# Two graph layers on one core: conv taps scaled one part ahead, a re-ordered beginning, and an own row for one channel of the early gates

## The chip, the cores and the metric

The kernel runs on one core of one Trainium2 chip. Its engines are TensorE (PE, with weight loads shown as PEld), VectorE (DVE), ScalarE (ACT), GpSimd (POOL) and SyncE (SP, which only issues transfers here). Each engine works through its own queue of instructions in order; semaphores tie the queues together. The time is device microseconds (us) of one execution; a kernel's time is the median of several.

## The reference

All arithmetic is float32. There are 64 graphs of 256 nodes with 256 features.

```python
# layer 0, then layer norm of x + result
deg = adj.sum(-1); deg = where(deg != 0, deg, 1)
a_plus = deg^-0.5[:, :, None] * adj * deg^-0.5[:, None, :] + alpha * eye
x = layernorm(x + (a_plus @ x) @ W.T + b)

# layer 1, then layer norm of x + result
h = relu(bn1(conv1x1(x)))                 # over channels
h = bn2(conv17(h))                        # 17 taps along the 256 nodes
x_conv = relu(h + x)
s = x @ w_se.T + b_se                     # 3 numbers per node
A = exp(-|s_n - s_m|^2) * adj             # the mask is adj
x_nmp = A @ relu(x @ w_msg.T + b_msg)
gi = concat(x_conv, x_nmp) @ w_ih.T + b_ih;  gh = x @ w_hh.T + b_hh
r, z = sigmoid(gi_r + gh_r), sigmoid(gi_z + gh_z)
n = tanh(gi_n + r * gh_n)
x = layernorm(x + (1 - z) * n + z * x)
```

## The kernel before

**Quarters.** The 64 graphs are worked off in four quarters of Q = 16. The 17-tap convolution is done in the frequency domain: each graph's h is cut into eight overlapping blocks of 48 nodes and transformed by a matmul (`p_dft`) into the tile `VM`, which holds 48 frequencies of 128 blocks, that is of 16 graphs. Then follow the products with the transformed taps (`products`, L559, one step for each of 12 pairs of frequencies, the `u` tiles loaded from memory), the inverse transforms on DVE (`real_transform`, `complex_begin`, `complex_end`), and stores to `xc_d`. After that the quarter's gates run: `gru` forms the gate products `p_g` (L893) from seven sums, and mixes and normalizes the result.

**One graph.** `layer0(g)` is a generator in pieces: degrees on ACT (L363), their power on POOL (L373, `dis`), adjacency transposed (`p_adjT`), the diagonal added on DVE (L387), x scaled (L402), `p_hT`, `p_out`, x<-p_out (L425), and `layernorm`: statistics and variance on DVE, a power on POOL (L329), `ln_mr` on DVE (L332), the normalization on ACT (L334). `layer1(g)` does the transposition of x (`p_x1T`), the 1x1 convolution (`p_conv`), `sq` and its sums on DVE (L467 to L470), `p_msg` and its ReLU, `p_dft`, `p_rows`, `p_dist`, exp on ACT (L521), the weighting `aT` on DVE (L524), and `p_nmp`. `graphs` interleaves: while graph i is in layer 1, graph i+2 is in layer 0 and i+3 begins it, and a third generator ("other") gets a turn at the places that `PLACES` names.

**What the third generator is.** In the first quarter it is `weights(n)`: thirteen parts of the conv taps, one for each of the first graphs. A part is loaded by seven transfers, multiplied by a scale on DVE (L300), transformed by eight matmuls (`p_u`, L308), evicted into `u_set`, subtracted on DVE (L313), added on POOL (L314), and stored to `ud` by three POOL transfers. In later quarters it is the gates of the quarter before: the first four graphs of a quarter ("early", `in_blocks`) run beside the last graphs of the next quarter, the others beside its first graphs and the transforms.

**Early gates.** `transposed(g)` brings the convolution's output into channel order: for early gates and the last quarter DVE transposes it in blocks (L838), POOL adds x (L839), POOL sets the row of x's first channel back to 1 (L840), and ACT applies the ReLU with bn2's bias (L842). That row (channel 0 of `xn`) holds 1 so that biases can ride in the matmuls; before L839 the true channel 0 is loaded over it by SP (L813).

**What sets the order.** A scheduler lays out each engine's queue from the order in which the program is written and from data dependencies. `with tc.issue_after(i):` keeps what is built inside behind instruction i where both are on the same engine. `paced` hands out pieces of one generator behind marked instructions of another. Each tile comes from a pool of a few buffers, so an allocation waits for the release of an older one. In the built program the transfers of SP and ACT share eight completion semaphores: the ninth transfer waits for the first, which holds the issuing queue.

**The beginning.** Loads of graph 0, the batch-norm vectors and graph 1 are issued; `layer0(0)` and `layer0(1)` are merged; `tables` fills the transform's tables by many small DVE copies and 12 transfers; then `batch_norms` makes bn1's and bn2's scales, spreads them by six matmuls with diagonals (`p_norm`, L187) and scales `wc1`.

Of the kernel before, what the change touches and what calls it, by code (L numbers as in the profile page):

```python
# [26 lines left out]
def kernel(  # L27
# [76 lines left out]
    def load(g):  # L104
        if g >= B:
            return
        ain[g] = loads.tile([P, NCH, N], F32, name="adj_t")
        nc.sync.dma_start(ain[g], adj[g].rearrange("(c p) m -> p c m", p=P))
        xin[g] = loads.tile([P, NCH, D], F32, name="x_t")
        nc.sync.dma_start(xin[g], x[g].rearrange("(c p) f -> p c f", p=P))  # L110

# [15 lines left out]
    nc.scalar.copy(warm, neg_half)  # L127
    for i, a in enumerate((bn1_g, bn2_g, bn1_b, bn2_b, bn1_m, bn2_m, bn1_v, bn2_v)):
        (nc.sync if i % 2 else nc.scalar).dma_start(vectors[2 * i : 2 * i + 2], a.rearrange("(c p) -> c p", p=P))
    nc.scalar.dma_start(w0, w0T.rearrange("(k p) o -> p k o", p=P))  # L130
    load(1)
# [31 lines left out]
    bn2_bias = const.tile([P, DCH], F32)  # L163

    def batch_norms(pool):
# [10 lines left out]
        nc.vector.tensor_mul(g, g, v)  # L176
        nc.vector.tensor_mul(m, m, g)
        nc.vector.tensor_sub(b, b, m)
        nc.vector.tensor_copy(bn2_bias, b[:, 2:4])

        ones = pool.tile([P, P], F32, name="ones")
        nc.vector.memset(ones, 1.0)
        rows = [bank("p_norm") for _ in range(2)]
        for i, col in enumerate((g[:, 0:1], g[:, 1:2], b[:, 0:1], b[:, 1:2], g[:, 2:3], g[:, 3:4])):
            diagonal = pool.tile([P, P], F32, name="diagonal", bufs=2)
            nc.vector.tensor_scalar(diagonal, ident, col, None, op0=ALU.mult)
            nc.tensor.matmul(rows[i // 4][:, i % 4 * P : (i % 4 + 1) * P], ones, diagonal, start=True, stop=True)  # L187
# [4 lines left out]
        nc.vector.tensor_copy(wc1[0:1, 0, :D], rows[0][0:1, D:])  # L192
# [22 lines left out]
    def tables(pool):  # L215
# [12 lines left out]
        nc.gpsimd.memset(fwd, 0.0)  # L228
        for r in range(2):
            nc.vector.memset(fwd_row[:, :, 2 * r], 1.0)  # L230
# [9 lines left out]
        with tc.issue_after(DIAGONAL[0]):  # L240

            for r in range(2):
                nc.vector.memset(w_row[:, :, r, NF], (0.5, 1.0)[r])
# [7 lines left out]
        for j in range(GT // 2 + 2):  # L251

            first = NT * (j - 1) - PAD
            lo, hi = max(first, 0), min(first + FL, P)
            nc.sync.dma_start(fwd[lo:hi, j, :], fwd_row[:, lo - first : hi - first])

# [16 lines left out]
    TAPS_OF = {}  # L273

    def load_taps(pool, n):
# [17 lines left out]
        nc.sync.dma_start(tp[KT - 1 :], taps(GC - 1, TR, 1, 1))  # L293

    def weights(pool, n, scale):
# [4 lines left out]
        nc.vector.tensor_mul(tp, tp, scale[:KT].unsqueeze(1).to_broadcast([KT, ng, D]))  # L300
# [3 lines left out]
        for i in range(2):  # L304
# [7 lines left out]
            if i == 1:  # L312
                nc.vector.tensor_sub(us[3], us[1], us[0])  # L313
                nc.gpsimd.tensor_tensor(us[2], us[0], us[1], op=ALU.add)  # L314
                for d, u in zip(ud, (us[0], us[3], us[2])):
                    nc.gpsimd.dma_start(d[:, n * ng : (n + 1) * ng], u)
            yield

    def layernorm(y, eps=LN_EPS, normed=None):

        chunks = range(y.shape[1])
        st = small.tile([P, NCH, nc.vector.BN_STATS_DIM], F32, name="ln_st")
        mv = small.tile([P, NCH, nc.vector.BN_AGGR_DIM], F32, name="ln_mv")
        rs = small.tile([P, NCH], F32, name="ln_rs")
        for c in chunks:
            nc.vector.bn_stats(st[:, c, :], y[:, c, :])
            nc.vector.bn_aggr(mv[:, c, :], st[:, c, :])
        nc.vector.tensor_scalar(rs[:, : len(chunks)], mv[:, : len(chunks), 1], eps, None, op0=ALU.add)  # L328
# [3 lines left out]
        nc.vector.scalar_tensor_tensor(mr[:, : len(chunks)], mv[:, : len(chunks), 0], -1.0, rs[:, : len(chunks)], op0=ALU.mult, op1=ALU.mult)  # L332
# [16 lines left out]
    EVICTED, RELU, SQUARED, AGGREGATED, LAYER0 = {}, {}, {}, {}, {}  # L349
    ADJT, X1, X_SCALED, DIAGONAL = {}, {}, {}, {}  # L350


    def layer0(g):
# [19 lines left out]
        nc.gpsimd.tensor_tensor(dis, deg, neg_half[:, :NCH], op=ALU.pow)  # L373
        adeg = small.tile([P, NCH], F32, name="adeg")
        nc.vector.tensor_scalar(adeg, deg, alpha_t, None, op0=ALU.mult)
# [27 lines left out]
        nc.gpsimd.tensor_tensor(x_t, x_t, b0_t.unsqueeze(1).to_broadcast([P, NCH, D]), op=ALU.add)  # L403

        yield
        hT = work.tile([P, DCH, N], F32, name="hT", bufs=1)
# [23 lines left out]
        yield from layernorm(x1, normed=NORMED)  # L430
# [354 lines left out]
    GATE, CONV, SUMS, OWN = {}, {}, {}, {}  # L785
# [22 lines left out]
    def load_gate(g):  # L808
        inputs = GATE[g] = gate.tile([P, 3 * DCH, N], F32, name="inputs")
        nc.sync.dma_start(inputs[:, : 2 * DCH], xn_d[g])  # L810
        if in_blocks(g):
            with nc.allow_non_contiguous_dma("one channel"):
                nc.sync.dma_start(inputs[0:1, 0], x1_d[g // Q][g % Q][:, 0:1].rearrange("n d -> d n"))  # L813
# [19 lines left out]
    def transposed(g):  # L833
# [3 lines left out]
        if in_blocks(g):  # L837
            behind(nc.vector.transpose(xcT.rearrange("p k (s r) -> p k s r", r=RB), CONV.pop(g)))  # L838
            nc.gpsimd.tensor_tensor(xcT, xcT, inputs[:, 0 : 2 * DCH : 2 * DCH - 1], op=ALU.add)  # L839
            JOINED.append(nc.gpsimd.memset(inputs[0:1, 0], 1.0).ins)  # L840
            for k in range(DCH):
                nc.scalar.activation(xcT[:, k], xcT[:, k], AF.Relu, bias=bn2_bias[:, k : k + 1])  # L842
# [25 lines left out]
    def normed(g, part, y):  # L868
# [8 lines left out]
    def gru(g):  # L877
# [37 lines left out]
        if following:  # L915
            transposed(g + 1)
# [343 lines left out]
```

## Time and profile before

| what | us |
|---|---|
| median of three runs (2070.37 to 2078.38) | 2074.39 |
| the profiled execution | 2077.37 |
| its span | 2075.6 |
| PE busy in the span | 1993.8 |
| DVE, ACT, POOL busy | 1360.7, 972.6, 663.4 |
| first `p_conv` starts at | 34.10 |
| last matmul group starts at | 2062.01 |

A profile line of a time line gives start, duration, engine, source line, operation, output <- inputs, sizes and count; the bracket is the engine's idle time before it and what ended it. A line of the list of waits gives who waited for whom, total us, times and the longest. In both, a name stands for all buffers of that name.

### The profile page before, as it was taken

The page shows a single profiled execution, that of the slowest core. Times are in us where ns is not written, and L with a number is a line of the kernel's source. Part 1 is how long each engine was busy: PE and PEld are TensorE (multiplying, and loading weights), DVE is VectorE, ACT ScalarE, POOL GpSimd, SP SyncE. Part 2 cuts the span into 40 slices and gives each one's busy share as a digit, 9 for nine tenths or more (in the row PEclk, how much of TensorE's full clock was granted, in tenths as well). Part 3 has the DMA queues.
Part 4 walks back from the last instruction along what each step waited for, and adds up shares of the span by engine and source line. Part 5 has one row for each costly group of instructions (what it writes and reads, how often), then busy time and mean ns, then how long its engine had stood idle before and what let it go on. Part 6 is the DMA issues. An engine that isn't in the chain of part 4 may idle for free.

```text
span 2075.6 us, 26338 instructions
## 1 busy us (share of the span) xinstructions
PE 1993.8 (96%) x8157; PEld 1445.7 (70%) x8157; DVE 1360.7 (66%) x3192; ACT 972.6 (47%) x2283; POOL 663.4 (32%) x672
## 2 busy tenths in 40 slices
PE   6989999999999999999999999999999999999997
PEld 5877788888667766777777766677767865555554
DVE  5434457587456788764455778775444899977776
ACT  3656664477442234556654223456655223333333
POOL 3433421022432234223332224323232034434442
PEclk9999999999999999999999999999999999999999
DMA  3765656544437655343334664434333944543431
GB/s 103 235 187 173 182 189 221 178 148 159 111 111 220 188 145 148 112 127 105 120 97 154 214 191 128 116 126 138 97 87 92 298 128 124 146 104 99 97 89 58
DMA packets 268936, 298.04 MB, mean 144 GB/s; under 512 B 84192, under 2 KB 211252, under 8 KB 268798
## 3 DMA queue, kind: packets, MB, share of 16 engines
q1 hardware_dynamic: 208846, 200.37, 33.2%
q10 hardware_dynamic: 44480, 67.39, 9.1%
q0 software_dynamic: 15472, 28.61, 6.4%
q8 instruction: 66, 1.08, 0.2%
q14 instruction: 72, 0.59, 0.1%
HBM read 193.19 MB, written 103.06 MB: 143 GB/s over the span
## 4 chain that ended last, share of the span: by engine, by line
PE 75%; DVE 12%; DMA 5%; ACT 3%; issue 2%; SPq 1%; POOL 1%; ACTq 0%; POOLq 0%; DVEq 0%
PE p_g L893 34%; PE p_k L559 10%; PE p_nmp L533 5%; PE p_hT L410 5%; PE p_out L420 4%; PE p_conv L457 4%; PE p_msg L478 3%; PE p_dft L496 3%; PE p_u L308 2%; PE p_dist L520 2%; PE p_x1T L440 1%; DMA u<-ud 1%; DMA taps<-in_conv2T_dram 1%; DMA inputs<-x_d 1%; PE p_adjT L384 1%
## 5 line engine op out<-in xcount | busy, mean ns | idle before, releaser
L893 PE MATMUL p_g<-wall,sums 128*128 128x384 f32 x1536 | 533.8, 488 | 2.8 <-DVE G L918 1.7
L893 PEld LDWEIGHTS p_g<-wall,sums 128*128 128x128 f32 x1536 | 284.9, 190 | 187.9 <-issue 9.5
L893 PE MATMUL p_g<-wall,inputs 128*128 128x384 f32 x1152 | 405.4, 487 | 6.9 <-DVE G L911 6.9
L893 PEld LDWEIGHTS p_g<-wall,inputs 128*128 128x128 f32 x1152 | 216.7, 190 | 157.4 <-DVE G L911 12.8
L864 POOL TENSOR_TENSOR sums<-inputs 128x384 f32<-128x384 f32 x128 | 141.8, 1108 | 332.3 <-PE p_g L893 309.5
L329 POOL TENSOR_TENSOR ln_rs<-ln_rs,neg_half 128x2 f32<-128x2 f32 x129 | 96.5, 748 | 458.7 <-DVE ln_rs L328 331.0
L524 DVE TENSOR_TENSOR aT<-aT,adjT 128x512 f32<-128x512 f32 x64 | 46.1, 720 | 253.5 <-ACT aT L521 253.5
L559 PE MATMUL p_k<-u,VM 128*128 128x256 f32 x736 | 171.3, 383 | 3.7 <-DMA u<-ud 2.4
L403 POOL TENSOR_TENSOR x_t<-x_t,b_t 128x512 f32<-128x512 f32 x64 | 89.1, 1392 | 249.4 <-ACT x L402 178.5
L559 PEld LDWEIGHTS p_k<-u,VM 128*128 128x128 f32 x736 | 139.6, 192 | 26.8 <-ACT ab L605 3.1
L410 PE MATMUL p_hT<-adjT,x 128*128 128x256 f32 x512 | 128.5, 396 | 13.3 <-ACT x L402 11.8
L533 PE MATMUL p_nmp<-aT,msg 128*128 128x256 f32 x512 | 125.3, 389 | 13.8 <-DVE aT L524 13.8
L937 ACT ACTIVATE G<-G 128x512 f32<-128x512 f32 x128 | 80.5, 631 | 123.7 <-DVE G L962 86.4
L334 ACT ACTIVATE x_g<-x_g,ln_mr,ln_rs 128x256 f32<-128x256 f32 x128 | 70.0, 593 | 137.8 <-DVE ln_mr L332 133.5
L420 PE MATMUL p_out<-w,hT 128*128 128x256 f32 x512 | 123.7, 385 | 7.8 <-ACT hT L415 7.6
L457 PE MATMUL p_conv<-wc,xn 128*128 128x259 f32 x512 | 124.6, 385 | 1.1 <-issue 1.1
L478 PE MATMUL p_msg<-wmsg,xn 128*128 128x256 f32 x512 | 121.3, 379 | 0.0
L533 PEld LDWEIGHTS p_nmp<-aT,msg 128*128 128x128 f32 x512 | 98.9, 194 | 30.7 <-DVE aT L524 16.9
L420 PEld LDWEIGHTS p_out<-w,hT 128*128 128x128 f32 x512 | 96.2, 192 | 30.8 <-ACT hT L415 13.8
L410 PEld LDWEIGHTS p_hT<-adjT,x 128*128 128x128 f32 x512 | 93.3, 195 | 34.5 <-ACT x L402 17.9
L864 POOL TENSOR_TENSOR sums<-inputs,sums 128x384 f32<-128x384 f32 x64 | 79.0, 1234 | 116.2 <-PE p_g L893 115.7
L496 PE MATMUL p_dft<-fwd,h 128*128 128x240 f32 x512 | 114.3, 366 | 0.0
(163 smaller groups left out, 3496.3 us busy)
## 6 DMA issues: line engine op xcount, KB each, us to landing
u<-ud SPq DMA_DIRECT2D x284, 256.0 KB
xn_d<-xn ACTq DMA_DIRECT2D x64, 512.0 KB
inputs<-xn_d SPq DMA_DIRECT2D x64, 512.0 KB
ud<-u_set POOLq DMA_DIRECT2D x39, 480.0 KB, 5.4
adj_t<-in_adj_dram SPq DMA_DIRECT2D x64, 256.0 KB
x_t<-in_x_dram SPq DMA_DIRECT2D x64, 256.0 KB
x_d<-x ACTq DMA_DIRECT2D x64, 256.0 KB
xc_d<-VM SPq DMA_DIRECT2D x64, 256.0 KB
```

What stands on the lines that cost most here:

```text
L329: nc.gpsimd.tensor_tensor(rs[:, : len(chunks)], rs[:, : len(chunks)], neg_half[:, : len(chunks)], op=ALU.pow)
L403: nc.gpsimd.tensor_tensor(x_t, x_t, b0_t.unsqueeze(1).to_broadcast([P, NCH, D]), op=ALU.add)
L410: nc.tensor.matmul(p[:, k, :], x1[:, mc, k * P : (k + 1) * P], adjT[:, mc, 1 - mc : 3 - mc, :].rearrange("p n q -> p (n q)"), start=mc == ...
L420: nc.tensor.matmul(p[:, c, :], hT[:, k, c * P : (c + 1) * P], w0[:, k, :], start=k == 0, stop=k == DCH - 1)
L457: nc.tensor.matmul(p, x1T[:, k, c * P : (c + 1) * P], wc1[:, k, :], start=k == 0, stop=k == DCH - 1)
L478: nc.tensor.matmul(p[:, c, :], x1T[:, k, c * P : (c + 1) * P], wmsg[:, k, :], start=k == 0, stop=k == DCH - 1)
L496: nc.tensor.matmul(p[:, t0 * FL : t1 * FL], h[:, c, k * P : (k + 1) * P], fwd[:, first : first + t1 - t0, :].rearrange("p t f -> p (t f)") ...
L533: nc.tensor.matmul(p[:, k, :], msg[:, mc, k * P : (k + 1) * P], aT[:, mc].rearrange("p n q -> p (n q)"), start=mc == 0, stop=mc == NCH - 1,)
L559: nc.tensor.matmul(p[:, j * D : (j + 1) * D], v[:, k, :], u[:, k, :], start=k == 0 and j == 0 and not onto, stop=k == DCH - 1, skip_group_ ...
L864: nc.gpsimd.tensor_tensor(S[i], x, y, op=op)
L893: nc.tensor.matmul(p[:, : 3 * HD] if k == 0 else p[:, HD:], a[:, k], wall[:, b, k].rearrange("p t d -> p (t d)"), start=first and k == 0, ...
L937: nc.scalar.activation(rz, rz, AF.Tanh, scale=0.5)
```

## The change

- **Taps.** `weights(n)` scales part n+1 behind `aT` of graph n instead of part n at its own start; only part 0 is scaled by itself. The set's subtraction, addition and stores become a third piece, behind degrees and `dis` of graph n+3. The first part starts one place later. x of graph i+3 is loaded behind the last transfer of the taps; adjacency is loaded on its own.
- **Beginning.** Graph 1's adjacency is loaded before the batch-norm vectors, which go over ACT, POOL and SP; the batch norms' first half comes right after both graphs' degrees, with the diagonals in `VM`; the table fill stands behind the second graph's diagonal, its last part behind the scaling of `wc1`; graph 1's normalization moves into the first graph. Two biases go through a small tile and a POOL copy.
- **Layer norm.** `ln_mr` stands behind the next graph's `adeg`, one piece sooner than the normalization, which no longer waits for `sq`.
- **Early gates.** x's first channel is loaded into a row of its own and added on POOL (1 x 256); the row of ones stays; the bias of channel 0 is one less (`less_one`). The DVE transposition stands behind the latest `aT`, one piece of `gru` sooner, and the ReLU behind the latest exp.
- **First quarter.** The real transform and the beginnings of the complex one stand behind the graphs' `sq`, diagonal and `aT`.
- **Last graph.** Half of its first row of results is mixed before the last product, so that half is left behind it.

```diff
+    load_adj(1)
     for i, a in enumerate((bn1_g, bn2_g, bn1_b, bn2_b, bn1_m, bn2_m, bn1_v, bn2_v)):
-        (nc.sync if i % 2 else nc.scalar).dma_start(...)
+        (nc.scalar if i < 2 else nc.gpsimd if i < 5 else nc.sync).dma_start(...)
+    load_x(1)
...
+        with tc.issue_after(DIAGONAL[1]):
+            nc.vector.tensor_mul(g, g, v)
...
+            for i, col in enumerate((g[:, 0:1], g[:, 1:2], b[:, 0:1], b[:, 1:2], g[:, 2:3], g[:, 3:4])):
+                nc.vector.tensor_scalar(VM[:, i, :P], ident, col, None, op0=ALU.mult)
+        yield
...
+    def scaled(tp, scale):
+        nc.vector.tensor_mul(tp, tp, scale[:KT].unsqueeze(1).to_broadcast([KT, GW // NPARTS, D]))
...
         tp = TAPS_OF.pop(n)
-        nc.vector.tensor_mul(tp, tp, scale[:KT].unsqueeze(1).to_broadcast([KT, ng, D]))
+        if n == 0:
+            scaled(tp, scale)
...
+            if i == 1 and n + 1 < NPARTS:
+                with tc.issue_after(WEIGHED[n]):
+                    scaled(TAPS_OF[n + 1], scale)
+            yield
+        with tc.issue_after(ADEG[n + 3]), tc.issue_after(POWERS[n + 3]):
+            nc.vector.tensor_sub(us[3], us[1], us[0])
+            nc.gpsimd.tensor_tensor(us[2], us[0], us[1], op=ALU.add)
+            for d, u in zip(ud, (us[0], us[3], us[2])):
+                nc.gpsimd.dma_start(d[:, n * ng : (n + 1) * ng], u)
+        yield
...
+        with tc.issue_after(ADEG[first]) if first in ADEG else ExitStack():
+            nc.vector.scalar_tensor_tensor(mr[...], mv[...], -1.0, rs[...], op0=ALU.mult, op1=ALU.mult)
+        if normed is not None:
+            yield
...
-                nc.sync.dma_start(inputs[0:1, 0], x1_d[g // Q][g % Q][:, 0:1].rearrange("n d -> d n"))
+                nc.sync.dma_start(CHANNEL[g], x1_d[g // Q][g % Q][:, 0:1].rearrange("n d -> d n"))
...
-            behind(nc.vector.transpose(xcT.rearrange("p k (s r) -> p k s r", r=RB), CONV.pop(g)))
+            if g < B - Q:
+                with tc.issue_after(WEIGHED[max(WEIGHED)]):
+                    nc.vector.transpose(to, CONV.pop(g))
+            else:
+                behind(nc.vector.transpose(to, CONV.pop(g)))
...
-            JOINED.append(nc.gpsimd.memset(inputs[0:1, 0], 1.0).ins)
-            for k in range(DCH):
-                nc.scalar.activation(xcT[:, k], xcT[:, k], AF.Relu, bias=bn2_bias[:, k : k + 1])
+            JOINED.append(nc.gpsimd.tensor_tensor(xcT[0:1, 0], xcT[0:1, 0], CHANNEL.pop(g), op=ALU.add).ins)
+            with tc.issue_after(EXP[max(EXP)]):
+                for k in range(DCH):
+                    nc.scalar.activation(xcT[:, k], xcT[:, k], AF.Relu, bias=less_one[:, k : k + 1])
...
+        sooner = following and in_blocks(g + 1) and g < B - Q
+        if sooner:
+            transposed(g + 1)
         yield
-        if following:
+        if following and not sooner:
             transposed(g + 1)
...
-                    with tc.issue_after(EVICTED[first + i]), tc.issue_after(SQUARED[first + i]):
+                    with tc.issue_after(EVICTED[first + i]):
                         run(ENDS.pop())
...
+        norms = batch_norms(setup)
+        for stage in firsts:
+            next(stage)
+        next(norms)
...
+        run(take(firsts[0], 2))
+        with tc.issue_after(STATISTICS[0]):
+            next(firsts[1])
+            scale2 = next(norms)
+        run(firsts[0])
+        run(fill)
+        next(firsts[1])
+        ENDS[0] = firsts[1]
...
+                if step >= 4:
+                    with ExitStack() as behind_graphs:
+                        for done in (SQUARED, DIAGONAL, WEIGHED):
+                            behind_graphs.enter_context(tc.issue_after(done[max(done)]))
+                        run(take(real, 1))
+                        run(complex_begin(step))
```

## The prediction

> **What bounds the kernel now.** I read the busy totals first, then the list of what TensorE (PE) waited for, then the time line of the worst places, engine by engine. Line numbers are those of the kernel before, unless a line is called new.
>
> ```profile
> span 2075.6 us, 26338 instructions
> PE 1993.8 (96%) x8157; PEld 1445.7 (70%) x8157; DVE 1360.7 (66%) x3192; ACT 972.6 (47%) x2283; POOL 663.4 (32%) x672
> ...
> PE p_nmp L533 <- DVE aT L524: 13.8, 7, 3.5
> PE p_hT L410 <- ACT x L402: 11.8, 15, 1.7
> PE p_out L420 <- ACT hT L415: 7.6, 8, 1.3
> PE p_adjT L384 <- DMA adj_t<-in_adj_dram: 7.2, 2, 5.1
> PE p_g L893 <- DVE G L911: 6.9, 6, 1.5
> PE p_norm L187 <- DVE bn L178: 6.3, 1, 6.3
> ```
>
> PE is busy for 1993.8 of 2075.6 us, and the change leaves its large matmuls alone. So only the 81.8 us in which PE stands still can be won, and what PE loses afterwards by a lower clock. By stretches the idle time is about 32 us before 300 us, 37 us from 300 to 1800, 1 us up to 2050 and 12 us at the end.
>
> The largest row, p_nmp behind aT, has its cause on VectorE (DVE). Its queue is in order, and the product of a part of the conv taps with the scale (L300) stands ahead of aT (L524):
>
> ```profile
> 113.70 2.33 DVE L300 TENSOR_TENSOR taps<-taps,scale 85x1024 f32<-85x1024 f32 x1 [7.13 <-DMA taps<-in_conv2T_dram]
> 115.96 0.68 DVE L524 TENSOR_TENSOR aT<-aT,adjT 128x512 f32<-128x512 f32 x1
> ...
> 102.90 1.92 PE L457 MATMUL p_conv<-wc,xn 128*128 128x259 f32 x8
> 116.69 3.78 PE L533 MATMUL p_nmp<-aT,msg 128*128 128x256 f32 x8 [3.15 <-DVE aT L524]
> 124.80 1.92 PE L457 MATMUL p_conv<-wc,xn 128*128 128x259 f32 x8
> 140.48 1.92 PE L457 MATMUL p_conv<-wc,xn 128*128 128x259 f32 x8
> ```
>
> From one graph's p_conv to the next is 15.68 us without the stall and 21.90 with it.
>
> **Part 1, taps a part ahead.** The scaling of part n+1 now stands behind aT of graph n, the seven loads of a part go out together ahead of x, and the subtraction and addition of the u sets (L313, L314) with their three stores move into the next graph, behind its degrees. PE's work is the same. Graph 1's p_conv starts at 51.27 and graph 12's at 247.73: 11 periods, 196.5 us, where 11 x 15.67 is 172.4. The excess is **24.1 us**.
>
> Here a rule bears on the size. The PE waits in that stretch are only 3.15 + 3.54 + 3.14 + 3.14 on aT and 1.34 on taps: 14.3 us. But after the first two, eight p_nmp matmuls took 3.78 us instead of 1.99. The Trainium skill ("TensorE: Matmul & The Clock Gate", What's actually happening) says the clock falls to half after an idle window of about 3.4 us and needs about as much work to come back. Waits alone would give 14, waits with the slow clock 24; I take the periods, which contain both.
>
> What can come back: taps landed as late as 113.5, 10.6 us after that graph's p_conv. Behind aT that is harmless until x<-p_out (L425, 10.5 us after p_conv) is several us late, since x is normalized only in the next graph. A second rule speaks against the move: "GPSIMD Engine Reference" (Key points) says GpSimd (POOL) shares SBUF interfaces with DVE, and the trace has L313 at 1.23 us alone and 3.37 when L314 began first. Now L313 stands ahead of the next sq (L467), whose result p_rows needs 5.5 us after p_conv. Starting at about 2.0 after p_conv, L313 ends at 3.2 or 5.4. In the second case p_rows and p_hT are some 0.85 us late in 12 graphs, 10 us together. Where ACT released both at once (48.64 and 63.85) DVE went first and took 1.23, so I take 1.23, and 3 us for late taps: **-21 us**, range -10 to -24.
>
> **Part 2, the new beginning.** Before, the first p_conv starts at 34.10:
>
> ```profile
> 10.89 6.74 PE L410 MATMUL p_hT<-adjT,x 128*128 128x256 f32 x16 [1.47 <-DVE adjT L387]
> ...
> 28.58 3.12 PE L187 MATMUL p_norm<-diagonal,ones 128*128 128x128 f32 x10 [6.33 <-DVE bn L178]
> ...
> 34.10 3.47 PE L457 MATMUL p_conv<-wc,xn 128*128 128x259 f32 x8 [1.12 <-issue]
> ```
>
> I walk the built order of the changed kernel with durations from these rows. adj of graph 0 lands at 5.1 as now; adj of graph 1 goes out third on SP, at about 1.8 instead of 5.4. The degree sums (0.8), pow on POOL (0.78) and scaled x (0.91) follow, with the table fill no longer in between: p_hT starts at 7.9 (10.89). Graph 1's scale, before held to 14.14 by the w_row fill, comes at 9.8, and p_hT, p_out, p_out of the two run through to 17.0. The batch-norm pow and the six diagonals are done by 13, so p_norm follows at once, 17.0 to 18.3. On DVE the fill (31 copies at 0.115, 3.6) comes between; x of graph 0 is added at 16.3 to 17.9, statistics to 19.0, pow to 19.8, wc scaled to 20.6, norm on ACT 20.8 to 21.9, four transposes and two evictions to 23.4. **p_conv at 23.5 to 25**, 9 to 10.6 sooner.
>
> Does what follows keep up? SP issues adj of graph 2 early, then six fwd stores (7.60 us for x6 in the trace) from 18 to 25.6, x of graph 2, and six wt loads (4.53 + 0.75) to 31. fwd is needed by p_dft at about 28.7, dft_w by p_u at 33.7 and ready at 33.2: both nearly tight. The taps of part 1 come behind them on SP and are needed only at 40. POOL carries three bn loads first (0.76 each), ident is ready near 4, before 5.1. **-9.5 us** (-5 to -12).
>
> **Part 3, the middle.** Four edits:
>
> - Early gates: the ReLU (L842, 2 x 0.5) moves behind exp. It sits on ACT ahead of hT and waits for POOL; seven p_out waits (1.33, 0.46, 1.33, 0.96, then 0.46, 1.17, 1.17 in the next quarter) have it in front, with the p_nmp waits of 0.22 and 0.50 behind: 7.6 us.
>
> ```profile
> 579.79 0.91 ACT L842 ACTIVATE inputs<-inputs,bn_bias 128x256 f32<-128x256 f32 x2 [2.79 <-POOL inputs L839]
> ...
> 580.72 0.58 ACT L415 COPY hT<-p_hT 128x512 f32<-128x512 f32 x1
> 581.35 1.99 PE L420 MATMUL p_out<-w,hT 128*128 128x256 f32 x8 [1.33 <-ACT hT L415]
> ```
>
> - Transposition behind aT, half a graph sooner. At 531.08 it waited 3.19 for its load, with sq, both diagonals and ln_mr behind: p_rows 1.32 and p_hT 1.71 late, and p_hT slowed from 1.99 to 3.15: 4.2 us. Behind aT a late load holds x<-p_out instead, which has slack.
> - The first quarter's real transform stands behind sq, diagonals and aT: at 402.74 and 404.86, 0.44 + 1.71 + 0.95: 3.1 us.
> - x1's first channel goes to a row of its own, so SP no longer waits for the load it would overwrite (7.4 us of SP, none of PE's). POOL does one 1x256 add where it did a 0.30 memset. The row does not show that add; POOL's smallest adds take 0.7, so +0.4 x 28 on an engine 32% busy: nothing on the path; 0.4 x 12 = 5 us if all the early gates waited for it.
>
> ln_mr now stands ahead of sq in all 64 graphs, behind the degrees. Where POOL's pow was early it costs nothing. Where it is late DVE now holds sq too: at 944.30 ln_mr had waited 1.18 and p_rows would be about 2.7 late. The page has 14 such waits, 9.7 us in all, gates' included; half of it on the path is 5 us. Sum: 7.6 + 4.2 + 3.1 - 5 = **-10 us** (-18 to 0).
>
> **Part 4, the end.** Before, from p5's add at 2064.61 to the last issue at 2071.49 is 6.9 us. The first half-row is now mixed earlier and the last holds 128 columns: five DVE steps and two tanh at about 0.2 less, statistics of half a row; but ln_mr of the other part still waits 0.77 on POOL ahead of the last subtraction. **-1.2 us** (-0.5 to -2).
>
> **Sum.** -21 - 9.5 - 10 - 1.2 = -41.7. The profiled execution took 2077.37 (span 2075.6 and 1.8 around it), so 2035.7; it lies 3.0 above the median 2074.39. For the median: **2032.7 us**.
>
> **Rivals.**
> (a) Transfers become the bound in the taps stretch. Per graph 256 + 256 + 512 + 256 + 3 x 480 + 340 KB = 3060 KB; in 15.67 us that is 200 GB/s. From 80 to 100 us the trace shows 221 GB/s at a DMA share of 0.73, which speaks against. If half the excess stays: 2045.
> (b) The middle gains nothing: ln_mr's new place and later gate sums give back 10: 2043.
> (c) Slower: ln_mr ahead of sq holds DVE on POOL's pow in the 36 graphs that carry gates (28 to 63). The case at 944 costs about 1.6 net, as p_g work lies between p_rows and p_hT. At 36 x 1.6 = 58 us against 46.7 of gains: 2086. It decides from 46.7 / 36 = 1.3 us per graph. Most ln_mr rows show no wait, so this is unlikely.
> (d) The beginning does not come forward, because fwd or dft_w are as late as now: 2042.
>
> **How the numbers follow.** Chances: forecast 0.62, (a) 0.12, (b) 0.12, (d) 0.08, (c) 0.06. About 0.5% (10.4 us) is what a measurement of this kernel can tell from no change. (a), (b) and (d) are still faster by more than that unless two meet; so faster 0.91, same 0.05, slower 0.04. The ends of all four parts are -33.5 - 22.5 = -56 (2018) and -15.5 (2059); all at one end is unlikely, so 2020 to 2052, which takes in (a), (b) and (d).
>
> **What would show it.** Right: p_conv starts near 24 and then every 15.7 us; no p_nmp wait before 300; L842's successor behind exp and p_out waits under 2 us in all; PE idle near 40. Wrong: p_rows waiting for ln_mr or sq, aT or L425 behind a taps wait with PE waiting too, p_u waiting for dft_w, or SP full.

## The result, and the profile after

The changed kernel takes 2042.89 us (median of four executions, 2039.88 to 2048.04) beside 2072.38 us for the kernel before on the same chip. The ratio is 0.9856, with a 95% interval from 0.9827 to 0.9884: 1.4% faster. The forecast said 2032.7, from 2020 to 2052. The time lies in the range, 10 us above the point.

The profile after is of the slowest of the four executions. First its page: span and busy totals.

```profile
span 2046.3 us, 26391 instructions
...
PE 1984.9 (97%) x8157; PEld 1437.7 (70%) x8157; DVE 1396.4 (68%) x3199; ACT 964.7 (47%) x2285; POOL 698.1 (34%) x679
```

PE stands still for 61.4 us instead of 81.8, and is busy 8.9 us less for the same 8157 matmuls, because fewer of them ran at a lower clock (the mean granted clock is 0.994 instead of 0.989). The list of what PE waited for shows which waits are gone:

```profile
PE p_g L930 <- DVE G L948: 12.2, 23, 1.5
PE p_adjT L414 <- DMA adj_t<-in_adj_dram: 5.5, 2, 5.2
PE p_x1T L470 <- ACT x L364: 4.5, 1, 4.5
PE p_k L589 <- DMA u<-ud: 3.7, 6, 1.3
PE p_conv L487 <- ACT xn L471: 3.5, 1, 3.5
PE p_g L930 <- POOL sums L901: 3.2, 2, 1.6
PE p_hT L440 <- ACT x L432: 2.3, 6, 0.5
...
PE p_nmp L563 <- DVE aT L554: 2.2, 3, 1.8
```

The wait for aT fell from 13.8 to 2.2 us, that of p_hT for x from 11.8 to 2.3, and p_out no longer appears (0.7 in all). But the first row has grown: the gate products wait 23 times for a sum on DVE, where they waited 6 times (6.9 us). That row is the main subject of what follows.

Waits do not contain what a stall costs in clock. So I compare by landmarks: starts of p_conv of graph 0, 1, 12, 15 and 63, start of the last group of p_g, and end of the span. The second column of results is another execution of the same changed kernel (run e5 below).

| stretch, us | before | after, first | after, e5 | forecast |
|---|---|---|---|---|
| start to graph 0 | 34.10 | 25.53 | 25.68 | -9.5 |
| graph 0 to 1 | 17.17 | 18.48 | 17.48 | |
| graph 1 to 12 | 196.46 | 180.57 | 175.21 | -21 with its neighbours |
| graph 12 to 15 | 37.77 | 42.25 | 40.65 | |
| graph 15 to 63 | 1310.59 | 1292.73 | 1291.49 | -10 |
| graph 63 to last p_g | 465.92 | 473.89 | 474.01 | 0 |
| last p_g to end | 13.59 | 12.85 | 12.78 | -1.2 |
| span | 2075.6 | 2046.3 | 2037.3 | -41.7 |

The three columns are single executions, and the spans fall by 29.3 and 38.3 us where the medians fall by 29.5. The one of before (2077.37) lies 5 us above its median, the first one after (2048.04) also 5 us above, that of e5 (2039.11) 3.5 us below. So some 5 us of the differences to before belong to that execution and can't be assigned to a stretch.

The beginning, on PE's time line of the changed kernel:

```profile
8.12 4.99 PE L440 MATMUL p_hT<-adjT,x 128*128 128x256 f32 x16
...
17.40 1.50 PE L198 MATMUL p_norm<-VM,ones 128*128 128x128 f32 x12
23.43 1.40 PE L470 MATMUL p_x1T<-ident,x 128*128 128x128 f32 x4 [4.53 <-ACT x L364]
25.53 3.79 PE L487 MATMUL p_conv<-wc,xn 128*128 128x259 f32 x8 [0.70 <-issue]
```

p_norm now needs no wait of its own (before: 28.58, after 6.33 of waiting); what remains is the wait for graph 0's normalization. And the taps' stretch, two graphs after the one stall that this execution had:

```profile
113.33 3.59 PE L487 MATMUL p_conv<-wc,xn 128*128 128x259 f32 x8 [3.52 <-ACT xn L471]
125.47 1.89 PE L563 MATMUL p_nmp<-aT,msg 128*128 128x256 f32 x8
130.66 1.91 PE L487 MATMUL p_conv<-wc,xn 128*128 128x259 f32 x8
141.12 1.89 PE L563 MATMUL p_nmp<-aT,msg 128*128 128x256 f32 x8
146.31 1.92 PE L487 MATMUL p_conv<-wc,xn 128*128 128x259 f32 x8
```

From 130.66 on a graph takes 15.65 us, and every p_nmp is at full speed (1.89, where the stalled ones of before took 3.78).

### The profile page after: what moved, and what is told of

Its sections match the earlier page's. It is cut to its first block, busy times and chain, and to the rows that moved or that the text cites. A ratio compares the mean times of both kernels' runs of the same rounds, so it can differ in the third digit from the quotient of the medians.

```text
span 2046.3 us, 26391 instructions
## 1 busy us (share of the span) xinstructions
PE 1984.9 (97%) x8157; PEld 1437.7 (70%) x8157; DVE 1396.4 (68%) x3199; ACT 964.7 (47%) x2285; POOL 698.1 (34%) x679
## 3 DMA queue, kind: packets, MB, share of 16 engines
q1 hardware_dynamic: 208842, 200.37, 33.8%
## 5 line engine op out<-in xcount | busy, mean ns | idle before, releaser
L901 POOL TENSOR_TENSOR sums<-inputs 128x384 f32<-128x384 f32 x128 | 143.1, 1118 | 329.0 <-PE p_g L930 303.2
L435 POOL TENSOR_TENSOR x_t<-x_t,b_t 128x512 f32<-128x512 f32 x64 | 101.9, 1592 | 215.3 <-ACT x L432 138.8
L977 ACT ACTIVATE G<-G 128x512 f32<-128x512 f32 (+1 forms) x129 | 81.0, 628 | 128.7 <-DVE G L1004 91.9
L901 POOL TENSOR_TENSOR sums<-inputs,sums 128x384 f32<-128x384 f32 x64 | 74.8, 1169 | 138.0 <-PE p_g L930 137.9
L487 PEld LDWEIGHTS p_conv<-wc,xn 128*128 128x128 f32 x512 | 99.1, 194 | 27.1 <-ACT xn L471 4.3
L950 ACT COPY G<-p_g 128x512 f32<-128x512 f32 x64 | 37.4, 584 | 155.9 <-PE p_g L930 107.2
```

Of the source, the lines that this page charges most:

```text
L487: nc.tensor.matmul(p, x1T[:, k, c * P : (c + 1) * P], wc1[:, k, :], start=k == 0, stop=k == DCH - 1)
L901: nc.gpsimd.tensor_tensor(S[i], x, y, op=op)
L977: nc.scalar.activation(rz, rz, AF.Tanh, scale=0.5)
```

## The experiments

Every run starts from the changed kernel. Ratios are to the kernel before, run beside it.

| run | what is set back | median us | ratio, 95% interval |
|---|---|---|---|
| e1 | own row, last quarter | 2033.28 | 0.9830 (0.9808 to 0.9853) |
| e2 | last part's pair of u sets | 2039.26 | 0.9858 (0.9841 to 0.9875) |
| e3 | gate-weight loads put last | 2046.16 | 0.9891 (0.9871 to 0.9911) |
| e4 | early gates' placement | 2045.08 | 0.9889 (0.9870 to 0.9908) |
| e5 | nothing | 2042.64 | 0.9851 (0.9829 to 0.9874) |
| e6 | own row everywhere | 2035.26 | 0.9813 (0.9794 to 0.9832) |
| e7 | order of the normalization | 2044.44 | 0.9860 (0.9839 to 0.9882) |
| e8 | first quarter's transform | 2040.06 | 0.9837 (0.9818 to 0.9856) |
| e9 | scaling and pairs of the taps | 2041.97 | 0.9859 (0.9844 to 0.9874) |
| e10 | pairs of the taps | 2047.31 | 0.9885 (0.9871 to 0.9900) |
| e11 | all of the middle, and own row | 2053.13 | 0.9908 (0.9891 to 0.9924) |
| e12 | three parts, where they cost | 2023.44 | 0.9769 (0.9754 to 0.9784) |

Executions of one kernel differ by 1 to 9 us, so an effect of 2 or 3 us is read from the landmarks. Single graphs and groups of a few repeat within 0.1 us in most runs; each stretch is of one execution.

### The last quarter: x1's first channel in its own row (e1, e6)

```diff
-        if in_blocks(g):
+        if g >= B - Q:
...
+                nc.sync.dma_start(inputs[0:1, 0], x1_d[g // Q][g % Q][:, 0:1].rearrange("n d -> d n"))
+        elif in_blocks(g):
             CHANNEL[g] = gate.tile([1, N], F32, name="channel", bufs=1)
...
+            if g >= B - Q:
+                JOINED.append(nc.gpsimd.memset(inputs[0:1, 0], 1.0).ins)
+                for k in range(DCH):
+                    nc.scalar.activation(xcT[:, k], xcT[:, k], AF.Relu, bias=bn2_bias[:, k : k + 1])
+                return
```

> Changed kernel, but in the last quarter x1's first channel is loaded over row 0 of the inputs again, and memset and ReLU stand as before; the early gates keep the row of their own. Theory (own row): the add on POOL no longer waits for the channel's transfer, so it runs on top of DVE's mixing and its ReLU stands ahead of the copy of first; undone, the last quarter takes about 9.5 us less (17 graphs at 13.5 instead of 14.0) and the time is about 2033 to 2035, 1.8 to 1.95% under before; PE's waits for G fall from 12.2 us to about 7. Rival (another edit, such as the order of the normalization or DVE's load): the quarter stays at 14.0 per graph, 2041 to 2045.

The last quarter takes 465.92 us, as before the change; with the row it took 473.80 to 478.63 in nine executions, two of the changed kernel and seven of others here that keep the row. The theory holds. PE's wait for that sum on DVE falls to 7.8 us in 8 waits. The mechanism is on three engines' time lines. Changed kernel:

```profile
1834.23 2.20 PE L930 MATMUL p_g<-wall,inputs 128*128 128x384 f32 x6 [0.20 <-DVE G L948]
...
1840.98 1.43 POOL L875 TENSOR_TENSOR inputs<-inputs 128x512 f32<-128x512 f32 x1 [1.45 <-DMA inputs<-xn_d]
1841.20 1.75 DVE L989 SCALAR_TENSOR_TENSOR G<-G 128x512 f32<-128x512 f32 x1
1842.43 0.51 ACT L879 ACTIVATE inputs<-inputs,less_one 128x256 f32<-128x256 f32 x1 [2.67 <-POOL inputs L875]
1842.48 1.05 POOL L876 TENSOR_TENSOR inputs<-inputs,channel 1x256 f32<-1x256 f32 x1
1842.85 0.57 ACT L941 COPY first<-p_g 128x512 f32<-128x512 f32 x1
1843.56 0.51 ACT L879 ACTIVATE inputs<-inputs,less_one 128x256 f32<-128x256 f32 x1
1843.98 0.61 ACT L993 ACTIVATE G<-G 128x512 f32<-128x512 f32 x1
```

Run e1, one graph at the same place in its loop:

```profile
1805.55 0.68 DVE L997 SCALAR_TENSOR_TENSOR G<-G 128x512 f32<-128x512 f32 x1
1806.27 0.63 ACT L1001 ACTIVATE G<-G 128x512 f32<-128x512 f32 x1 [0.98 <-DVE G L997]
...
1809.03 1.27 POOL L878 TENSOR_TENSOR inputs<-inputs 128x512 f32<-128x512 f32 x1 [5.15 <-DMA inputs<-x_d]
```

And the kernel before, where the ReLU followed at 1855.43:

```profile
1850.93 0.63 ACT L953 ACTIVATE G<-G 128x512 f32<-128x512 f32 x1 [0.99 <-DVE G L949]
...
1854.13 1.27 POOL L839 TENSOR_TENSOR inputs<-inputs 128x512 f32<-128x512 f32 x1 [5.58 <-DMA inputs<-x_d]
```

In e1, as before, POOL's add waits for the channel's transfer, 5.15 us here, and in that time DVE and ACT finish the mixing. Without that wait the add starts in the middle of the mixing. DVE's step next to it takes 1.75 instead of 0.68 us, and on ACT both halves of the ReLU stand ahead of the tanh that the mixing needs, which starts 1.03 us after its input is ready (at 1842.95). Counted from the start of PE's group before it, DVE's loop is 2.05 us later. In e1 it had 1.7 to spare (its sum ends at 1810.51, PE needs it at 1812.24). So PE now waits 0.20 us a graph; the interval of two groups with that wait is 2.30 instead of 1.94, the next 2.04 instead of 1.94, and a graph takes 14.02 instead of 13.54. Which of the two delays would be enough alone was not separated. Run e1 also takes out POOL's extra add (1.05 us at 1842.48). PE does not wait for what that add delays on POOL: it waits for POOL's sums twice in the whole execution, with the row and without it (3.2 us both times).

For the early gates the question was the opposite one: did the row carry part of the middle's gain?

```diff
-            CHANNEL[g] = gate.tile([1, N], F32, name="channel", bufs=1)
...
-                nc.sync.dma_start(CHANNEL[g], x1_d[g // Q][g % Q][:, 0:1].rearrange("n d -> d n"))
+                nc.sync.dma_start(inputs[0:1, 0], x1_d[g // Q][g % Q][:, 0:1].rearrange("n d -> d n"))
...
-                    nc.scalar.activation(xcT[:, k], xcT[:, k], AF.Relu, bias=less_one[:, k : k + 1])
+                    nc.scalar.activation(xcT[:, k], xcT[:, k], AF.Relu, bias=bn2_bias[:, k : k + 1])
```

> Changed kernel with the first channel loaded over row 0 of the inputs for the early gates too, not for the last quarter alone. Theory (forecast: SP's 7.4 us of waiting was hidden, so the row of its own brings PE nothing in the middle): equal to the run that undid the last quarter alone, 35 to 36 us under before. Rival (the middle gained 19 us where 10 were forecast, and the placement gave only some 2 of it, so the row carries it): 5 to 8 us above that run, lost in graphs 28 to 31, 44 to 47 and 60 to 63.

Graphs 15 to 63 took 1294.6 us, against 1290.1 to 1292.8 in the five executions with the whole middle in place (first, e1, e2, e3, e5). So the row is worth some 2.7 us there, no more than these five differ among themselves: between the forecast's nothing and the rival's 5 to 8. In the ratios (0.9813 here, 0.9830 in e1) no loss shows.

### The taps (e2, e9, e10)

Run e2 puts the pair of the last part back behind its second set:

```diff
+            if i == 1 and n == NPARTS - 1:
+                nc.vector.tensor_sub(us[3], us[1], us[0])
+                nc.gpsimd.tensor_tensor(us[2], us[0], us[1], op=ALU.add)
+                for d, u in zip(ud, (us[0], us[3], us[2])):
+                    nc.gpsimd.dma_start(d[:, n * ng : (n + 1) * ng], u)
             yield
+        if n == NPARTS - 1:
+            return
```

> Changed kernel, but the subtraction and addition of the u sets of the last part of the taps, with their stores, stand in graph 12 again, behind the second set; the other parts are left. Theory (the pair ahead of sq stretches DVE's small operations in graph 13, where no p_u covers it): graph 13 takes about 12.3 instead of 16.4 us, the whole 4 us less, about 2039. Rival (slow clock or gate weights): graph 13 stays above 15.5 and the time at 2043.

Graph 13 fell to 12.64 us, where the changed kernel took 16.43 and, in five other executions (e1, e4, e5, e6, e8), 14.81 to 14.83. The theory holds; its size was read from the one execution that also had the slow clock. In the changed kernel:

```profile
239.35 1.21 DVE L339 TENSOR_TENSOR u_set<-u_set,u_set 120x1024 f32<-120x1024 f32 x1
239.81 2.97 POOL L340 TENSOR_TENSOR u_set<-u_set,u_set 120x1024 f32<-120x1024 f32 x1
240.49 2.32 DVE L497 SCALAR_TENSOR_TENSOR sq<-scols 128x6 f32<-128x6 f32 x1
...
243.12 2.69 DVE L417 SCALAR_TENSOR_TENSOR adjT<-ident,adeg,adjT 128x128 f32<-128x128 f32 x2
...
245.95 2.61 PE L440 MATMUL p_hT<-adjT,x 128*128 128x256 f32 x6 [1.67 <-DVE adjT L417]
```

DVE did go first (1.21), as the forecast took it, but what follows on DVE is held as long as POOL's adds run: a product of 6 columns takes 2.32 instead of 0.17. The two diagonals take 2.69 instead of 0.61 and end 0.17 us after POOL's next add (L435, 244.37 to 245.64). They began 1.25 us before that add and at their usual speed would have been over by then; why they still stood is not shown. In graphs 1 to 12 the pair stands beside 3.2 us of p_u ahead of p_conv and is over when sq comes. After the last part there is no p_u.

Run e9 does so for every part, and scales each part at its own start:

```diff
-        if n == 0:
-            scaled(tp, scale)
+        scaled(tp, scale)
...
-            if i == 1 and n + 1 < NPARTS:
-                with tc.issue_after(WEIGHED[n]):
-                    scaled(TAPS_OF[n + 1], scale)
```

> Changed kernel with the taps of each part scaled and the pair of u sets taken in the part's own graph again; loads, beginning and the rest stay. Theory (forecast: scaling a part ahead is worth 21 us): graphs 1 to 12 take some 196 us instead of 175 and the time is 18 to 20 above the changed kernel (graph 13 gets its 2.6 us back), 2060 to 2063. Rival (the loads of a part going out together ahead of x are what frees the stretch): under 6 us, below 2049.

The theory fell; the time is what the rival said. Graphs 1 to 12 took 179.6 us, of 196.5 before and 175.2 in e5. So 16.9 of the 21.3 us remain with the scaling and the pairs back in their own graph. Of the missing 4.4 us, 1.6 lie in graph 1: the pair's addition on POOL holds the scaling on DVE there (3.38 us at 57.73 instead of 1.22), and p_u waits 1.34 for it. The other 2.8 lie in graphs 3 and 4, where late transfers held ACT's queue for 1.55 and 3.14 us, as they did in other executions too (next section). Graph 2 and graphs 5 to 11 took 15.65 or 15.66, as in e5. So scaling ahead, with the pair behind it, is worth between 1.6 and 4.4 us. Run e9 shows why it is so little:

```profile
118.45 1.22 DVE L314 TENSOR_TENSOR taps<-taps,scale 85x1024 f32<-85x1024 f32 x1
123.22 0.69 DVE L557 TENSOR_TENSOR aT<-aT,adjT 128x512 f32<-128x512 f32 x1 [3.55 <-ACT aT L554]
...
124.50 1.89 PE L566 MATMUL p_nmp<-aT,msg 128*128 128x256 f32 x8
```

The scaling stands ahead of aT, as before, but its taps are there: it runs 4.4 us after that graph's p_conv (114.03), where before it came 10.8 after. What e9 keeps of the change is the order of the transfers, the seven of a part together and x behind them, the earlier start of SP's queue, and the first part one place later. What frees the stretch is among these; which of them by how much was not separated.

Run e10 keeps the scaling a part ahead and sets only the pairs back, all of them:

```diff
-            if i == 1 and n == NPARTS - 1:
+            if i == 1:
```

> Changed kernel with scaling a part ahead, but the pair of every part in its own graph, behind its second set, as the run before this did for the last part alone. Theory (the forecast's fear, POOL and DVE stretching each other, decides where the pair stands: behind aT it meets only the scaling and x<-p_out, which have slack): the same as with the last part alone, graphs 1 to 12 in 175 us, 2 us under the changed kernel. Rival (scaling and pair together hold x<-p_out and the statistics): 0.5 to 3 us more in each of 12 graphs, 2046 to 2075.

The theory fell and the rival held: graphs 1 to 12 took 183.6 us, and from graph 2 on a graph took 16.34 instead of 15.65. Run e10:

```profile
73.05 2.38 POOL L339 TENSOR_TENSOR u_set<-u_set,u_set 120x1024 f32<-120x1024 f32 x1 [2.84 <-ACT u_set L333]
73.14 3.37 DVE L314 TENSOR_TENSOR taps<-taps,scale 85x1024 f32<-85x1024 f32 x1
...
76.56 3.28 PE L330 MATMUL p_u<-taps,dft_w 85*120 85x256 f32 x14 [0.42 <-DVE taps L314]
```

The pair's addition starts on POOL 0.09 us ahead of the scaling on DVE, which then takes 3.37 instead of 1.22, and the next p_u waits 0.42 for it. So once the scaling is behind aT, the pair has to leave it: the two edits belong together.

### The stall in graphs 4 and 5 (e3, e5)

```diff
+                with tc.issue_after(TAPS_OF["last"]):
                     nc.sync.dma_start(wall[:, b, 0, 0:1], own[:, 2:3, at])
                     nc.sync.dma_start(wall[:, b, 0, 1:3], own[:, 0:2, at])
...
```

> Changed kernel, but the loads of the gate weights go out on SP behind the last load of taps, not in between from graph 3 on. Theory (a late gate-weight load holds ACT's queue for a shared completion semaphore): the wait of 4.93 us on ACT in graph 4 is gone, graphs 4 and 5 take 15.7 each instead of 19.3 and 17.3, the whole 5 us less, about 2038. Rival (the transfers of taps, adj and x themselves are the bound there): the stall only moves or stays, 2043; a third outcome is that the 16 loads together hold x of graphs 13 to 15, which gives it back.

> The changed kernel once more, as the measure for the runs beside it. If the stall in graphs 4 and 5 is of the kernel, graph 4 to 6 takes 36.7 us again and the time is near 2046; if it is of that one execution, 31.3 and 2039 to 2042. Graph 13 (16.4 us) and the last quarter (14.0 us a graph) should come again in both.

In its full size the stall was of that one execution: without any edit, e5 took 31.3 us from graph 4 to 6 instead of 36.7. But it comes and goes: e1, e2, e5 and e12 took 31.3 as well, while e4, e6, e7, e8, e9 and e11 took 31.7 to 33.8, each with ACT waiting for a gate-weight load there (0.95 us in e7 to 2.69 in e4). In e12 ACT waited too (0.98), without a loss. So e3, at 31.3, can't show that its edit removed anything. It shows that the wait came with the loads, to graph 11. On ACT's time line, the changed kernel first:

```profile
111.93 0.34 ACTq L568 DMA_DIRECT2D xn_d<-xn  x1
112.32 0.42 ACT L393 ACTIVATE adjT<-adj_t 128x256 f32<-128x256 f32 x1 [4.93 <-DMA wall<-in_w_hhT_dram]
```

and run e3:

```profile
219.76 0.42 ACT L393 ACTIVATE adjT<-adj_t 128x256 f32<-128x256 f32 x1 [2.77 <-DMA wall<-in_w_ihT_dram]
```

L393 does not read gate weights. It stands behind a store in ACT's queue, and what let the queue go on was, by the trace, the landing of a gate-weight load on SP. The reading is that the store had to wait for one of the shared completion semaphores, which that load still held; why the load was late is not shown. In e3 p_conv of graph 12 then waited 1.35, and graphs 1 to 12 took 1.5 us more than in e5; graph 13 took 3.3 more with the slow clock (last section).

### The middle (e4, e7, e8, e11)

Run e4, in `gru` and `transposed`; the early gates also get their old number of turns:

```diff
-        sooner = following and in_blocks(g + 1) and g < B - Q
+        sooner = False
...
-                with tc.issue_after(WEIGHED[max(WEIGHED)]):
-                    nc.vector.transpose(to, CONV.pop(g))
+                behind(nc.vector.transpose(to, CONV.pop(g)))
...
-            with tc.issue_after(EXP[max(EXP)]):
```

> Changed kernel with the early gates' work placed as before: transposition after the second step, not behind aT; ReLU not behind exp; the paces of the early gates as before. The channel's own row, the order of the normalization and the first quarter's transform are kept. Theory (the forecast's items): 7.6 + 4.2 = 11.8 us come back, about 2055, with p_out waits on hT of some 7 us in all. Rival (the normalization's new order carries the middle's gain): under 4 us come back, 2043 to 2047.

Run e7, with the extra turn of layer 0 taken out as well:

```diff
-        yield from layernorm(x1, normed=NORMED, first=g + 1)
+        yield from layernorm(x1, normed=NORMED)
...
-                    with tc.issue_after(EVICTED[first + i]):
+                    with tc.issue_after(EVICTED[first + i]), tc.issue_after(SQUARED[first + i]):
```

> Changed kernel with ln_mr and the normalization behind sq again, as before. Theory (forecast: ln_mr ahead of sq gives back 5 us): some 5 us faster than the changed kernel, about 2037. Rival (the new order gains: graphs 36 and 52 are each 1.2 us shorter after the change, and p_rows no longer waits for ln_mr): 5 to 9 us slower, 2047 to 2051.

Run e8:

```diff
-                run(merge(products(step), take(real, 1 if q else 0)))
-                if q:
-                    run(complex_begin(step))
+                run(merge(products(step), take(real, 1)))
+                run(complex_begin(step))
...
-                        for done in (SQUARED, DIAGONAL, WEIGHED):
```

> Changed kernel with the first quarter's real transform and the begin of the complex one beside the products again, not behind sq, the diagonals and aT. Theory (forecast): 3.1 us come back, 2045 to 2046, at graph 19 (15.9 us becomes 19.8). Rival (the gain at graph 19 is given back in graphs 20 to 28, which got 3.05 us longer): graph 19 loses 3.8, graphs 20 to 28 win 3, and the time is the same, 2042 to 2043.

Run e11 is the three together, with the row of e6.

> Changed kernel with all of the middle undone together: placement of the early gates, row of the first channel (the last quarter's too), order of the normalization and the first quarter's transform. Theory (the single undos gave back 2 us each because they are covers of the same few waits): all together give back the middle's whole 19 us, less the 8 that the last quarter wins: 2052 to 2055. Rival (something else of the change, such as the order of POOL's add to x or the degrees' transfer, made the middle shorter): 2036 to 2045.

Graphs 15 to 63, against the mean of 1291.9 us of the five executions named above (e9 and e10, which also have the whole middle, lie at 1292.2 and 1291.0): e4 1293.1 (+1.2), e6 1294.6 (+2.7), e7 1294.9 (+3.0), e8 1289.7 (-2.2). The five reach from 1290.1 to 1292.8, so e4 and e8 can hardly be told from no change. The four add up to 4.7 us. All together, e11, took 1312.3: +20.4, back at the 1310.6 of before, and e11's theory holds. Its list of waits says what the parts have in common:

```profile
PE p_hT L438 <- ACT x L430: 14.9, 18, 1.7
PE p_out L448 <- ACT hT L443: 9.2, 8, 2.1
```

Before, these two were 11.8 and 7.6 us. With one part taken out, e4, e6, e7 and e8 have 2.3, 5.4, 8.8 and 2.1 us for p_hT and 0.7 for p_out in each. So the single parts do not have prices of their own. They are covers of the same few waits; as long as the others stand, taking one away costs little, and only without all of them does the stretch go back. e4's theory (11.8 us) fell. So did both of e8's sides: graph 19, which was to lose 3.8 us, took 15.6. e7's rival has the sign right, with half its size.

The normalization's order is the part whose two sides are seen. Setting it back lengthened graphs 36 to 39 and 52 to 55 by 4.3 us each (67.5 to 71.8) and shortened graphs 20 to 27 by 3.0 (101.9 to 98.9). Of the 4.3 us, 2.0 lie in graph 36, where p_hT waits 1.71 for x on ACT in e7 and not in e5. The other 2.3 lie in graph 39, where p_g waits 2.25 instead of 1.61 for POOL's sums and the six matmuls behind it take 3.37 instead of 2.20 (granted clock 0.72 from 930 to 936 us). The price, the 3.0 us of graphs 20 to 27, is not on DVE, where the forecast sought it, but on ACT. Run e5:

```profile
414.03 1.09 ACT L364 ACTIVATE x<-x,ln_mr,ln_rs 128x256 f32<-128x256 f32 x2 [1.93 <-DVE ln_mr L360]
415.03 0.56 ACT L415 COPY adjT<-p_adjT 128x512 f32<-128x512 f32 x1
...
415.64 0.44 PE L539 MATMUL p_rows<-ident,scols 128*128 128x128 f32 x2 [0.25 <-ACT adjT L415]
...
416.61 0.70 PE L440 MATMUL p_hT<-adjT,x 128*128 128x256 f32 x2 [0.53 <-ACT x L432]
```

Run e7, the same graph:

```profile
411.61 0.58 ACT L413 COPY adjT<-p_adjT 128x512 f32<-128x512 f32 x1
413.15 1.09 ACT L362 ACTIVATE x<-x,ln_mr,ln_rs 128x256 f32<-128x256 f32 x2 [0.96 <-DVE ln_mr L360]
414.76 0.38 PE L537 MATMUL p_rows<-ident,scols 128*128 128x128 f32 x2
```

The normalization (1.09 on ACT, after a wait of 1.93) now stands ahead of the copy of the adjacency, so the copy and x scaled are late, and PE waits 0.25 and 0.53. Where graphs carry nothing else for PE, nothing hides it.

### Three parts set back where they cost (e12)

```diff
+    OLD = {*range(15, 29), *range(33, 36), *range(49, 52)}
-        yield from layernorm(x1, normed=NORMED, first=g + 1)
+        yield from layernorm(x1, normed=NORMED, first=None if g in OLD else g + 1)
...
+                    behind_sq = first + i + 1 in OLD
-                    with tc.issue_after(EVICTED[first + i]):
+                    with tc.issue_after(EVICTED[first + i]), tc.issue_after(SQUARED[first + i]) if behind_sq else ExitStack():
```

The edits of e1 and e2 are in it too.

> Changed kernel with three parts set back where they cost: the last quarter's channel over row 0, the last part's pair of u sets in graph 12, and the old order of the normalization where it was dearer (graphs 15 to 28, 33 to 35, 49 to 51). Theory (the three add up): 8 + 2.2 + 4.5 to 6 us under the changed kernel, about 2027, ratio to before 0.977 to 0.979. Rival (the gains overlap, or a late graph shifts the gates behind it): 2031 to 2035, no better than with the channel alone.

2023.44 us, ratio 0.9769: 2.3% under before, and the fastest kernel here. The stretches show that the three add up: graph 13 takes 12.65, graphs 20 to 27 98.9, graphs 36 to 39 still 67.5, the last quarter 464.8. Its median lies 16.7 under what e5's ratio makes of the same before (0.9851 x 2071.01 = 2040.2), a little more than the 14.7 to 16.2 expected.

## Why the prediction was right, and where it was not

The total came out inside the range, and part of that is luck. The last quarter's 8 us and graph 13's 2.2 or more were not in the forecast. By the table, what paid for them is the middle, which gained 8 to 9 us more than its wrongly priced items said.

- **Taps, -21: the size was right, the cause was not.** Graphs 1 to 12 gave back 21.25 us in e5 (15.9 in the first execution, with its stall). The step "the scaling of part n+1 now stands behind aT" was given all of it. By e9 it is worth 1.6 to 4.4 together with the moved pair. At least 16.9 come with what e9 keeps, the transfers first of all, which the forecast listed and did not price: taps that land by the time of the old scaling leave no wait to move. So the size was met by luck.
- **The port rule, weighed at 10 us and set aside.** In the twelve graphs that it was weighed for it cost nothing as the change places the pair; beside the scaling it would have cost 0.7 us a graph (e10). It came in the thirteenth, where no p_u covers the pair: 2.2 us by e2, up to 3.8 with the slow clock. The row chosen (DVE first, 1.21) was right for L339 and said nothing of the small steps behind it, which have to stand until POOL's 2.97 are over.
- **Beginning, -9.5: measured -8.6.** p_hT (7.9, measured 8.12) and p_norm (17.0, measured 17.40) came as walked. The mis-sized term is the table fill on DVE, 3.6 us: its copies ran from 11.64 to 18.9, since three of its small copies took 1.2 to 1.3 us instead of 0.2 beside POOL's adds. x of graph 0 was added at 18.22 instead of 16.3, the norm came at 22.78 instead of 20.8.
- **Middle, -10: measured -17.9 and -19.1.** The items (7.6 for the ReLU, 4.2 for the transposition, 3.1 for the transform, -5 for ln_mr) were read from single waits and summed. Undone alone, the first two gave back 1.2, the third nothing, and the last 3.0 where it was to cost 5. The waits were the right ones and nearly all went; what failed is that each had one owner.
- **The last quarter, 0: it lost 8 us, and this is the step that failed.** "+0.4 x 28 on an engine 32% busy: nothing on the path" priced the new POOL instruction and not what the row of its own releases: POOL's add had been waiting for the channel (5.58 us at 1854.13 before), and that wait kept it clear of DVE's mixing and kept the ReLU behind the tanh on ACT. The price of the instruction was too low as well: the 1x256 add took 1.05 us, not 0.7. Together with the taps' thirteenth graph this is what the forecast lacks.
- **End, -1.2: measured -0.7 to -0.8.**
- **Rivals.** (a) Transfers as the bound: not so in e5, where the excess is gone; the first execution's stall of 5 us came from a late gate-weight load that held ACT's queue. (b) The middle gains nothing: no. (c) ln_mr holds DVE in every gate graph: no, the order gained in graphs 36 to 39 and 52 to 55. (d) The beginning stays: no.

## What to carry to other kernels

When an edit takes a wait away, list what that wait kept apart: the instruction that now comes early shares ports and queues with new neighbours, and an engine that is a third busy can still arrive at the one bad moment of a tight loop. Several edits against the same waits do not have prices that add; undo them one at a time and all together before saying which of them earned the gain. And when a consumer waits for a transfer, look first at what is queued ahead of that transfer before moving the consumer.

## What the runs showed of the hardware that was not expected

- **DVE does not run slower beside POOL's add, it stands until the add is over.** L497 (6 columns, 2.32 us) ends at 242.81 and POOL's L340 beside it at 242.78; L989 ends 0.54 after POOL's L875. In e5, L360 (128x2, both inputs in SBUF) began 58 times while POOL formed one of its sums (L901), with 0.33 to 0.94 us of that left, and ended 0.01 to 0.02 after it each time. L986 (128x512) did so 34 times, with 0.22 to 0.39 left, and ended 0.55 to 0.56 after it. The Trainium skill ("SBUF — State Buffer", SBUF: two separate sides) states this as a lock: the first of the two engines holds the shared ports for its whole instruction, and only DVE steps with two inputs in SBUF, or in a two-port mode, need them. The rows agree on both points: in e1, under POOL's add at 1809.03 (1.27), the aggregation L354 with one input kept its 0.16 at 1809.05, and a DVE sum of `first` and `p_g`, whose second input is a matmul's result, took its usual 0.65 at 1809.13. On POOL's side the measurement differs: its power (L403, 128x2, 0.70 us) held none of the 46 steps of L360 that began under it in e5 (0.15 to 0.16 each). So the price of meeting an addition is what is left of POOL's instruction, however small the step is.
- **A transfer can hold an engine that never uses its data**: 4.93 us on ACT for a gate-weight load of SP, in one of two executions of the same kernel, and 2.69, 2.47 and 2.77 in e4, e8 and e3.
- **The same wait is not always followed by the slow clock.** In e5 and in e3 PE waits about 0.56 and 1.66 us at the same two places of graph 13. In e5 p_out then takes 1.89; in e3 the clock drops, p_out takes 3.51, and the graph 18.08 instead of 14.81. Two stretches of each show it (time, busy times of PE, PEld, DVE, ACT and POOL, granted clock, transfer share, GB/s). First e5:

```profile
230.00:245.00 15.00, 12.78 (x65) 10.28 (x64) 9.21 (x17) 8.66 (x24) 7.18 (x7) 1.00 0.57 186
245.00:260.00 15.00, 14.41 (x72) 11.73 (x71) 9.85 (x35) 9.39 (x26) 3.45 (x3) 1.00 0.59 195
```

and e3, with a clock of 0.93 and 0.84 where e5 has 1.00:

```profile
230.00:245.00 15.00, 12.78 (x57) 10.14 (x57) 9.39 (x17) 8.23 (x24) 7.18 (x7) 0.93 0.81 274
245.00:260.00 15.00, 14.41 (x62) 11.49 (x58) 6.90 (x28) 8.23 (x24) 3.45 (x3) 0.84 0.45 135
```

Of the seven executions with these two waits (first, e1, e3, e4, e5, e6, e8), two have the slow clock behind them, first and e3. The idle window that the forecast's rule names does not tell them apart, and what decides it is not settled here.
